# Rounding scales and normalisations as SCALAR_TENSOR_TENSOR, zeros written by ScalarE, and another order of the steps between two stages

## The chip, the cores and the metric

The kernel runs on one core of a Trainium2 chip. The core has five engines, each with its own instruction queue: TensorE (PE, matrix products; its weight loads are listed as PEld), VectorE (DVE), ScalarE (ACT), GpSimd (POOL) and SyncE (SP, which issues DMA transfers). They share the on-chip memory SBUF and the accumulation banks PSUM, and wait for one another by semaphores. The metric is the device time of one execution in microseconds; lower is better.

## The reference

Two layers in post-norm form on x of shape 16 x 512 x 256, float32 throughout. Reduced to what matters:

```python
x = layernorm(x + attention(x))        # 16 heads, latent size 32, rotary, causal softmax
x = layernorm(x + fp4_ffn(x))          # silu(gate) * up, then down; width 704
x = layernorm(x + recurrence(x))       # 512 steps of tanh(state @ tanh(a) + x_t @ b)
x = layernorm(x + channel_mix(x))      # sigmoid gate, squared relu

def fp4_quant_dequant(x):              # on activations and on weights, blocks of 16
    scale = maximum(max(abs(xb), axis=-1) / 6.0, 1e-12)
    idx = searchsorted(MID, abs(xb / scale))
    return GRID[idx] * sign(xb / scale) * scale

def layernorm(x):
    return (x - mean(x)) / sqrt(var(x) + 1e-5)
```

## The kernel before

**Stage 1, attention and FFN.** It goes through 16 batches. A batch has twelve slots: four groups of heads by three blocks of queries. A slot's chain is: scores on PE (L524), mask and row minimum on DVE in one operation (L536, which writes `p` and `nm`), exp on ACT (L549), transposes on PE (L559), copies to SBUF on ACT (L561), the weighted sum on PE (L590), and a division (L573, L604 to L611). Between the slots of one batch, other steps are taken from a list written by hand (`PLAN`, with variants for batches 0, 1 and 15; `Beside.half_slot` takes them): latents and rotary products of the next batch (L457, L473, L476), the output projection of the batch before with its layernorm (`out_projection`), and that batch's FFN: rounding of the rows (`quantize`), gate and up products (`ffn_up`), rounding of the hidden rows, and the down product with its layernorm (`ffn_down`). All of it works on blocks of 128 rows; a batch has four.

**Order.** PE's order is that in which the program is written (`tc.manual_schedule` for PE). The orders of DVE, ACT, POOL and SP are made by a scheduler, from data dependences and from costs, so an instruction that is taken out or costed in another way moves its neighbours. PSUM banks rotate over a pool of seven.

**fp4 rounding** (`fp4`, L183 to L215) is called 142 times: 74 times on 256 columns of activations or weights with 128 rows, twice with 64 rows, and 66 times on 704 columns. Its operations are: L201 the block maxima, L202 the scale with its lower bound, L203 the reciprocal, L204 a factor 1 - 2^-23 on the reciprocal, L207 the product with the rows, L209 and L210 the exponent, L213 the addition that rounds (all DVE), and L214 the subtraction and L215 the product with the scale (POOL). The buffers `q_sc`, `q_inv`, `q_q`, `q_m` exist twice.

**Layernorm.** `stats_into` (L91, L92, DVE) gives mean and variance, `rstd_of` (L84, L86, POOL) the factor, and one DVE instruction with two values for each row subtracts and multiplies: L98 in `layernorm` (after the FFN, 64 times) and L502 in `out_projection` (after the attention, 64 times, in pairs).

**Between the stages.** After the last slot only batch 15's output projection and FFN are left, and stage 2 cannot begin before its first rows are done. `FIRST` is a list of steps that sets PE's order there: E quantizes the rows of a block (`quantize_now`), U is one call of `ffn_up` (transposes, then two halves of the products), D one of `ffn_down`, F takes one DVE step of a hidden block's rounding, N is `normed`, the RMS norm and transposes of the recurrence's first rows. The number is the block (or pair).

**Stage 2** is the recurrence: 512 steps, PE products L1020 and L1060, tanh on ACT into `hist` (L1068), with channel mix, read-out and the last layernorm of earlier rows beside it.

**Zeroed buffers.** `vpad` (two of 128x2048, L400) is zeroed by POOL in the prologue, `hist` (four of 128x1024, L1008) by POOL at the start of the transition. `ta` (128x1024) holds tanh(a) and is ready long before.

Of the kernel before, what the change touches and what calls it, by code (L numbers as in the profile page):

```python
# [10 lines left out]
F32 = mybir.dt.float32  # L11
# [3 lines left out]
AF = mybir.ActivationFunctionType  # L15
ALU = mybir.AluOpType
# [3 lines left out]
P = 128  # L20
B, T, C = 16, 512, 256
# [38 lines left out]
def tile_kernel(ctx: ExitStack, tc: tile.TileContext, I: dict, out: bass.AP):  # L60
    nc = tc.nc


    const = ctx.enter_context(tc.tile_pool(name="const", bufs=1))
# [3 lines left out]
    make_identity(nc, ident)  # L68
    neg_half = const.tile([P, 4], F32, name="neg_half")
    nc.gpsimd.memset(neg_half, -0.5)  # L70
    cols = const.tile([P, NCOLS], F32, name="cols")
    nc.sync.dma_start(cols, I["cols"])

# [7 lines left out]
    def rstd_of(mv, n, eps):  # L81

        ve = small.tile([P, 4], F32, tag="ve", name="ve")
        nc.gpsimd.tensor_scalar(ve[:, :n], mv[:, :n, 1], 1.0, eps, ALU.mult, ALU.add)  # L84
        rs = small.tile([P, 4], F32, tag="rstd", name="rstd")
        nc.gpsimd.tensor_tensor(rs[:, :n], ve[:, :n], neg_half[:, :n], ALU.pow)  # L86
        return rs

    def stats_into(mv_slice, x):
        st = small.tile([P, 6], F32, tag="bnst", name="bnst")  # L90
        nc.vector.bn_stats(st, x)  # L91
        nc.vector.bn_aggr(mv_slice, st)  # L92

    def layernorm(dst, src):
        mv = small.tile([P, 4, 2], F32, tag="mv", name="mv")
        stats_into(mv[:, 0, :], src)
        rs = rstd_of(mv, 1, LN_EPS)
        nc.vector.tensor_scalar(dst, src, mv[:, 0, 0:1], rs[:, 0:1], ALU.subtract, ALU.mult)  # L98

# [46 lines left out]
    def mm(name):  # L148
        banks.append(banks.pop(0))
        return banks[-1].tile([P, 512], F32, tag="mm", name=name)  # L150
# [30 lines left out]
    def fp4(dst, x, nb, rows=P):  # L181

        n = nb * 16
        sc = ffn.tile([P, 44], F32, tag="q_sc", name="q_sc", bufs=2)[:rows, :nb]  # L190
        inv = ffn.tile([P, 44], F32, tag="q_inv", name="q_inv", bufs=2)[:rows, :nb]
        q = ffn.tile([P, FF], F32, tag="q_q", name="q_q", bufs=2)[:rows, :n]
        m = ffn.tile([P, FF], F32, tag="q_m", name="q_m", bufs=2)[:rows, :n]

        def blocks(t):
            return t.rearrange("p (n k) -> p n k", k=16)

        def over(t):
            return t.unsqueeze(2).to_broadcast([rows, nb, 16])

        nc.vector.tensor_reduce(sc, blocks(x), AX.X, ALU.max, apply_absolute_value=True)  # L201
        nc.vector.tensor_scalar(sc, sc, 1.0 / 6.0, 1e-12, ALU.mult, ALU.max)  # L202
        nc.vector.reciprocal(inv, sc)  # L203
        nc.vector.tensor_scalar(inv, inv, 1.0 - 2.0**-23, None, ALU.mult)  # L204
        if n > C:
            yield
        nc.vector.tensor_tensor(blocks(q), blocks(x), over(inv), ALU.mult)  # L207
        yield
        nc.vector.tensor_scalar(m.bitcast(U32), q.bitcast(U32), 0x7F800000, None, ALU.bitwise_and)  # L209
        nc.vector.tensor_scalar(m, m, 1.0, 1.5 * 2.0**22, ALU.max, ALU.mult)  # L210
        if n > C:
            yield
        nc.vector.tensor_tensor(q, q, m, ALU.add)  # L213
        nc.gpsimd.tensor_tensor(q, q, m, ALU.subtract)  # L214
        nc.gpsimd.tensor_tensor(blocks(dst), blocks(q), over(sc), ALU.mult)  # L215

    def ffn_weights():
# [20 lines left out]
        for r in range(2):  # L238
            w = ffn.tile([P, FF], F32, tag="h", name="w", bufs=2)
            nc.sync.dma_start(w, I["w_down"][r * P : r * P + P, :])  # L240
            wq4 = ffn.tile([P, FF], F32, tag="hq", name="wq4", bufs=2)
            for _ in fp4(wq4, w, FF // 16):
                pass
            yield 0.3
            for k0 in (0, 3):
                ps = mm("ps_t")
                for kb in range(k0, k0 + 3):
                    (of, n), at = PARTS[kb], (kb - k0) * P
                    nc.tensor.transpose(ps[:n, at : at + P], wq4[:, of : of + n], ident)
                    nc.scalar.copy(wdT[:n, kb, r * P : r * P + P], ps[:n, at : at + P])  # L250
                yield 1.5
# [89 lines left out]
    with ExitStack() as a:  # L341
# [54 lines left out]
            )  # L396

        vpad = [wts.tile([P, NT, H, 32], F32, name=f"vpad{i}") for i in range(2)]
        for i in range(2):
            nc.gpsimd.memset(vpad[i], 0.0)  # L400

# [78 lines left out]
        def out_projection(b):  # L482
            while b not in whole:
                yield None
            x, yT = x_of[b], y_of.pop(b)
            for j in range(0, NT, 2):
                mv = small.tile([P, 4, 2], F32, tag="mv", name="mv")
                ps = mm("ps_o")
                for i in range(2):
                    for hf in range(2):  # L490
                        nc.tensor.matmul(
                            ps[:, i * C : i * C + C],
                            yT[:, hf, (j + i) * P : (j + i) * P + P], cpT[:, hf, :],
                            start=hf == 0, stop=hf == 1,
                        )
                both = x[:, j : j + 2, :].rearrange("p j c -> p (j c)")
                nc.vector.tensor_tensor(both, ps, both, ALU.add)
                for i in range(2):
                    stats_into(mv[:, i, :], x[:, j + i, :])
                rs = rstd_of(mv, 2, LN_EPS)  # L500
                for i in range(2):
                    nc.vector.tensor_scalar(  # L502
                        x[:, j + i, :], x[:, j + i, :], mv[:, i, 0:1], rs[:, i : i + 1],
                        ALU.subtract, ALU.mult,
                    )
                yield 0.9

# [190 lines left out]
        with tc.manual_schedule(engines={mybir.EngineType.PE}), ExitStack() as s:  # L698
# [8 lines left out]
            rows = prep.tile([1, C], F32, name="rows")  # L707
# [74 lines left out]
        ps_b = five.enter_context(tc.tile_pool(name="ps_b", bufs=5, space=PSUM))  # L782
        ps_y = five.enter_context(tc.tile_pool(name="ps_y", bufs=1, space=PSUM))
        banks[:] = [ps_2] * 2 + [ps_b] * 5

        with tc.manual_schedule(engines={mybir.EngineType.PE}):
            slots = [(b, g, n) for b in range(B) for g in range(4) for n in range(len(BLOCKS))]
# [3 lines left out]
            for slot in slots + [None]:  # L791
                if slot:
                    b, g, n = slot
                    if g == 0 and n == 0:
# [5 lines left out]
                        if b == 2:  # L800
                            ta, wb, wc, bout = recurrent_weights()
# [176 lines left out]
    def value(p):  # L978
# [24 lines left out]
    hist = [  # L1003
        [wts.tile([P, 8, 2, 64], F32, name=f"hist{g}{i}") for i in range(2)] for g in range(2)
    ]
    for g in range(2):
        for i in range(2):
            nc.gpsimd.memset(hist[g][i], 0.0)  # L1008
    state = [None, None]
    clean, ot_of = {}, {}  # L1010

# [63 lines left out]
    def beside(M):  # L1075
# [14 lines left out]


    FIRST = [
        "E3", "U0", "U0", "E1", "U0", "U3", "U1", "U1", "D0", "E2", "F0", "D0", "U1", "U2", "N0",
        "U2", "U3", "F1", "U2", "N0", "F2", "U3",
    ]
    LATER = {
        0: [
# [23 lines left out]
    with tc.manual_schedule(engines={mybir.EngineType.PE}):  # L1121
# [40 lines left out]
        for t in range(T):  # L1162
# [9 lines left out]
            for g in range(2):  # L1172
                if us[g] is None or us[g][0] + us[g][1] == t:
                    t0, n = starts[g].pop(0)
# [9 lines left out]
            if t % 8 == 7:  # L1184
                at = t % 16 - 7
                for g in range(2):
                    old, new = hist[g][t // 8 % 2], clean[t // 16, g]
                    old = old.rearrange("p t k (r s b) -> p t k r s b", r=2, s=2)
                    for r in range(2):
                        rs, qs = slice(r * 64, r * 64 + 64), slice(64 - r * 64, 128 - r * 64)  # L1190
# [108 lines left out]
```

## Time and profile before

| | us |
|---|---|
| median of 3 runs | 2560.16 (2558.01 to 2562.15) |
| profiled execution, its own time | 2558.65 |
| its span in the profile | 2556.6 |
| prologue, up to the first scores | 31.0 |
| batches 0 and 1 | 98.7 and 111.1 |
| batches 2 to 14, each | 107.6 to 109.6 |
| batch 15 | 110.6 |
| transition, up to the recurrence's first product | 67.1 |
| recurrence | 728.3 |

A batch is counted from its first score product (L524) to that of the next; batch 15 ends, and the transition begins, with the last score product of all.

How to read the rows: a group of instructions has its line, engine, operation, output and inputs by the program's names, the shape, the number of instructions (x), then busy time in us, mean ns of one, and the idle time of the engine ahead of them with what ended it. A row of the timeline has the start in us, the length in us (of all its instructions, where there are several), engine and line; in brackets stands the engine's idle time before it and the instruction that released it. Instructions of one engine overlap at their ends, so the time from start to start can be shorter than the length.

### The profile page before, as it was taken

Reading aid. Unit: us, or ns where it says so; the run is one execution under the profiler, and the core shown is the slowest. Engines: PE = TensorE matmul, PEld = TensorE weight load, DVE = VectorE, ACT = ScalarE, POOL = GpSimd, SP = SyncE. Lnnn points to the kernel's source line nnn. Section 1 sums busy time; section 2 is a strip of 40 time slices with the busy share of each in tenths; the row PEclk is TensorE's granted clock in tenths of the full one; section 3 lists DMA queues with packets and bytes.
Section 4 is the critical chain, followed back from the end, with each engine's and each line's share of the span. In section 5 each row is a group of like instructions: output and inputs, shape, how many; then the busy total and the mean of one; then the engine's idle time right before and its main releaser. Section 6 shows DMA issues by size and latency. Waiting matters only on the chain.

```text
span 2556.6 us, 73922 instructions
## 1 busy us (share of the span) xinstructions
PE 2428.8 (95%) x28802; PEld 1713.3 (67%) x28802; DVE 1944.7 (76%) x5621; ACT 1613.2 (63%) x5532; POOL 1036.7 (41%) x1649
## 2 busy tenths in 40 slices
PE   8789999999999999999999999997799999999998
PEld 4456666666666666666666666665578888888885
DVE  6767888788888888888787887877756666666666
ACT  4656666666666666667666666664266666666664
POOL 4322333333333333333333333333545555555554
PEclk9889999999999999999999999999899999999999
DMA  3000000000000000000000000000101111111100
GB/s 118 22 10 6 14 22 14 16 15 12 24 14 16 16 12 24 14 16 14 14 16 22 14 14 7 16 11 11 42 28 40 40 40 40 38 38 40 36 28 27
DMA packets 58016, 61.30 MB, mean 24 GB/s; under 512 B 7873, under 2 KB 53058, under 8 KB 57666
## 3 DMA queue, kind: packets, MB, share of 16 engines
q1 hardware_dynamic: 56802, 55.54, 7.1%
q8 instruction: 226, 3.70, 0.6%
q14 instruction: 124, 1.02, 0.1%
q10 hardware_dynamic: 864, 1.05, 0.1%
HBM read 39.79 MB, written 16.78 MB: 22 GB/s over the span
## 4 chain that ended last, share of the span: by engine, by line
PE 54%; DVE 28%; ACT 9%; POOL 5%; issue 3%; DMA 1%; ACTq 0%; DVEq 0%; POOLq 0%
PE u L1060 8%; DVE p L536 6%; PE ps_pt L559 5%; PE u L1020 5%; PE S L524 4%; ACT p L549 4%; PE py L590 3%; PE pg L160 3%; PE pu L160 3%; PE ps_h L439 3%; ACT pT L561 3%; DVE q_q L207 2%; PE ps_a L904 2%; PE ps_d L160 2%; DVE q_sc L201 2%
## 5 line engine op out<-in xcount | busy, mean ns | idle before, releaser
L549 ACT ACTIVATE p<-p,nm 128x512 f32<-128x512 f32 (+3 forms) x1024 | 569.9, 561 | 520.1 <-DVE nm L536 516.1
L1068 ACT ACTIVATE hist<-u 64x64 f32<-64x64 f32 x2048 | 445.5, 218 | 235.1 <-PE u L1060 153.0
L536 DVE CUSTOM_DVE_ANT_0 p<-S,mask 128x512 f32<-128x512 f32 (+3 forms) x1024 | 443.7, 483 | 50.2 <-PE S L524 50.2
L559 PEld LDWEIGHTS ps_pt<-ident,p 128*128 128x128 f32 x2560 | 296.5, 141 | 235.4 <-issue 85.5
L1060 PEld LDWEIGHTS u<-hist,ta 128*64 128x64 f32 x8176 | 367.3, 138 | 119.9 <-ACT hist L1068 40.7
L559 PE MATMUL ps_pt<-ident,p 128*128 128x128 f32 x2560 | 393.3, 280 | 9.0 <-DVE nm L536 3.5
L1060 PE MATMUL u<-hist,ta 128*64 128x32 f32 x8176 | 394.2, 218 | 4.6 <-ACT hist L1068 4.4
L561 ACT COPY pT<-ps_pt 128x384 f32<-128x384 f32 (+1 forms) x768 | 370.0, 515 | 39.2 <-PE ps_pt L559 38.9
L214 POOL TENSOR_TENSOR q_q<-q_q,q_m 128x256 f32<-128x256 f32 (+1 forms) x142 | 167.3, 1178 | 452.0 <-DVE q_q L213 434.4
L524 PE MATMUL S<-kc,qr 32*128 32x128 f32 (+3 forms) x2048 | 235.3, 474 | 8.9 <-ACT qr L478 7.9
L1020 PE MATMUL u<-xt,wb 128*64 128x64 f32 x4128 | 223.0, 230 | 2.4 <-issue 2.4
L549 ACT ACTIVATION_READ_ACCUMULATOR p<-p,nm 128x1 f32 x1024 | 199.3, 195 | 0.0
L160 PE MATMUL pg<-wgT,xqT 128*128 128x352 f32 x512 | 177.6, 470 | 4.1 <-ACT xqT L289 2.9
L473 POOL TENSOR_TENSOR qc<-qc,qs 128x512 f32<-128x512 f32 x64 | 81.5, 1274 | 236.3 <-DVE qs L472 231.3
L160 PE MATMUL pu<-wuT,xqT 128*128 128x352 f32 x512 | 172.8, 460 | 1.2 <-DVE th L304 1.2
L160 PE MATMUL ps_d<-wdT,hT 128*128 128x256 f32 x732 | 169.7, 381 | 2.2 <-ACT hT L323 2.2
L590 PEld LDWEIGHTS py<-pT,vpad 128*32 128x32 f32 x5120 | 141.2, 110 | 43.0 <-issue 30.7
L1020 PEld LDWEIGHTS u<-xt,wb 128*64 128x64 f32 x4128 | 164.9, 138 | 7.4 <-issue 3.0
L590 PE MATMUL py<-pT,vpad 128*32 128x128 f32 x5120 | 165.3, 276 | 3.8 <-ACT pT L561 3.5
L524 PEld LDWEIGHTS S<-kc,qr 32*128 32x128 f32 x2048 | 110.8, 185 | 78.0 <-issue 32.0
L84 POOL TENSOR_SCALAR ve<-mv 128x1 f32<-128x1 f32 (+1 forms) x160 | 32.6, 204 | 302.1 <-DVE mv L92 276.7
L160 PEld LDWEIGHTS ps_d<-wdT,hT 128*128 128x128 f32 x732 | 134.9, 191 | 19.6 <-ACT hT L323 3.1
(164 smaller groups left out, 4595.6 us busy)
## 6 DMA issues: line engine op xcount, KB each, us to landing
xT<-in_xT_dram SPq DMA_DIRECT2D x16, 512.0 KB
x<-in_x_dram SPq DMA_DIRECT2D x16, 512.0 KB
xs<-x SPq DMA_DIRECT2D x64, 128.0 KB
x<-xs SPq DMA_DIRECT2D x32, 256.0 KB
xm<-xs SPq DMA_DIRECT2D x32, 256.0 KB
out_dram<-o SPq DMA_DIRECT2D x64, 128.0 KB
w<-in_w_down_dram SPq DMA_DIRECT2D x2, 352.0 KB
w<-in_w_gate_dram SPq DMA_DIRECT2D x5, 128.0 KB
```

The source lines that it names most:

```text
L160: nc.tensor.matmul(dst, left, right, start=start, stop=stop)
L214: nc.gpsimd.tensor_tensor(q, q, m, ALU.subtract)
L473: nc.gpsimd.tensor_tensor(of[k], of[k], x, ALU.add)
L524: nc.tensor.matmul(S[h][:, at : at + w], q[rs, i * P : i * P + P], k[rs, :w], start=True, stop=True,)
L536: nc.vector.tensor_tensor_reduce(out=p[:, own], in0=S[h][:, own], in1=mask[:, T - (i + 1) * P :], scale=1.0, scalar=-MASKED, op0=ALU.add, ...
L549: nc.scalar.activation(p[:, own], p[:, own], AF.Exp, bias=nm[:, u : u + 1], scale=-1.0, accum_out=sum_of[b, g][:, cb, half, h : h + 1],)
L559: nc.tensor.transpose(ps[:, at : at + P], p[:, at : at + P], ident)
L561: nc.scalar.copy(pT[:, :w], ps[:, :w])
L590: nc.tensor.matmul(py[q * 32 : q * 32 + 32, PLACE[i][1], :], vpad[b % 2][:, j, g * 4 + h, :], pt, start=j == 0 and h % 2 == 0, stop=j == i ...
L1020: nc.tensor.matmul(u[rs, k, par:n:2, bs : bs + 16], wb[:, g * 2 + k, par, half, rs], xt[:, g, at : at + n - par : 2, :], start=par == 0 an ...
L1060: nc.tensor.matmul(into[cs, :, c, :], ta[:, t % 2, g * 2 + k, cs], own[:, :, c, :], start=False, stop=True, skip_group_check=True,)
L1068: nc.scalar.activation(state[g][rs, :, r * 32 : r * 32 + 32].rearrange("p k (s b) -> p k s b", s=2), u[rs, :, t - t0, :] .rearrange("p k ( ...
```

## The change

1. In `fp4`, L202 becomes a SCALAR_TENSOR_TENSOR whose second operand is a constant tile `tiny` (128x44, set to 1e-12 once by POOL). L204 is taken out; its factor goes into L207, which becomes a SCALAR_TENSOR_TENSOR.
2. In `layernorm` and `out_projection` the TENSOR_SCALAR with two values for each row becomes a SCALAR_TENSOR_TENSOR: the mean as the per-row scalar, the factor as a tensor broadcast along 256 columns.
3. `vpad` is zeroed after the prologue's preparation in program order; on POOL this puts the small zeroing of `ones` ahead of it.
4. `hist` is zeroed by four ACT instructions: Identity of `ta` with scale 0.
5. `FIRST` has another order, with the same steps.

On the engines: DVE has 142 instructions fewer, POOL three fewer (four zeroings gone, one new), ACT four more; PE and SP have the same number. PE's order differs in the transition alone, SP's in one pair of loads of the prologue that change places. DVE's order differs around each rounding; the ACT and POOL orders differ by a few places for each batch.

```diff
@@
+    tiny = const.tile([P, 44], F32, name="tiny")
+    nc.gpsimd.memset(tiny, 1e-12)
@@ layernorm
-        nc.vector.tensor_scalar(dst, src, mv[:, 0, 0:1], rs[:, 0:1], ALU.subtract, ALU.mult)
+        nc.vector.scalar_tensor_tensor(
+            dst, src, mv[:, 0, 0:1], rs[:, 0:1].to_broadcast([P, C]), ALU.subtract, ALU.mult
+        )
@@ fp4
         nc.vector.tensor_reduce(sc, blocks(x), AX.X, ALU.max, apply_absolute_value=True)
-        nc.vector.tensor_scalar(sc, sc, 1.0 / 6.0, 1e-12, ALU.mult, ALU.max)
+        nc.vector.scalar_tensor_tensor(sc, sc, 1.0 / 6.0, tiny[:rows, :nb], ALU.mult, ALU.max)
         nc.vector.reciprocal(inv, sc)
-        nc.vector.tensor_scalar(inv, inv, 1.0 - 2.0**-23, None, ALU.mult)
         if n > C:
             yield
-        nc.vector.tensor_tensor(blocks(q), blocks(x), over(inv), ALU.mult)
+        nc.vector.scalar_tensor_tensor(
+            blocks(q), blocks(x), 1.0 - 2.0**-23, over(inv), ALU.mult, ALU.mult
+        )
@@ before the attention's preparation
         vpad = [wts.tile([P, NT, H, 32], F32, name=f"vpad{i}") for i in range(2)]
-        for i in range(2):
-            nc.gpsimd.memset(vpad[i], 0.0)
@@ out_projection
-                    nc.vector.tensor_scalar(
-                        x[:, j + i, :], x[:, j + i, :], mv[:, i, 0:1], rs[:, i : i + 1],
-                        ALU.subtract, ALU.mult,
+                    nc.vector.scalar_tensor_tensor(
+                        x[:, j + i, :], x[:, j + i, :], mv[:, i, 0:1],
+                        rs[:, i : i + 1].to_broadcast([P, C]), ALU.subtract, ALU.mult,
                     )
@@ after the attention's preparation
         banks[:] = [ps_2] * 2 + [ps_b] * 5
+        for i in range(2):
+            nc.gpsimd.memset(vpad[i], 0.0)
@@ stage 2
     for g in range(2):
         for i in range(2):
-            nc.gpsimd.memset(hist[g][i], 0.0)
+
+            nc.scalar.activation(
+                hist[g][i].rearrange("p t k n -> p (t k n)"), ta.rearrange("p a k n -> p (a k n)"),
+                AF.Identity, scale=0.0,
+            )
@@
     FIRST = [
-        "E3", "U0", "U0", "E1", "U0", "U3", "U1", "U1", "D0", "E2", "F0", "D0", "U1", "U2", "N0",
-        "U2", "U3", "F1", "U2", "N0", "F2", "U3",
+        "U0", "U0", "E1", "E3", "U0", "U3", "D0", "U1", "F0", "E2", "D0", "U1", "N0", "U2", "U1",
+        "F1", "U2", "U2", "U3", "U3", "F2", "N0",
     ]
```

## The prediction

> **What bounds the kernel now.** I read the page's totals and its chain, then the windows by stage, then the groups of the edited lines with shapes kept apart, and last the timeline where those lines stand.
>
> ```profile
> span 2556.6 us, 73922 instructions
> PE 2428.8 (95%) x28802; PEld 1713.3 (67%) x28802; DVE 1944.7 (76%) x5621; ACT 1613.2 (63%) x5532; POOL 1036.7 (41%) x1649
> PE 54%; DVE 28%; ACT 9%; POOL 5%; issue 3%; DMA 1%; ACTq 0%; DVEq 0%; POOLq 0%
> ```
>
> PE is busy 95% of the span, yet only 54% of the chain is PE: the other half is DVE (28%), ACT and POOL handing work to it. A shorter DVE instruction pays where it stands on that 28%. The windows below are one steady batch, the transition, and the recurrence (columns: length; busy us of PE, PEld, DVE, ACT, POOL; PE clock; DMA share; GB/s).
>
> ```profile
> 893.00:1001.00 108.00, 106.02 (x852) 70.78 (x853) 89.01 (x267) 71.13 (x213) 37.35 (x45) 1.00 0.05 16
> 1761.00:1828.00 67.00, 45.05 (x254) 31.18 (x246) 45.96 (x124) 13.94 (x42) 24.68 (x35) 0.87 0.09 28
> 1828.00:2557.00 729.00, 704.75 (x15206) 569.71 (x15206) 483.94 (x1253) 466.71 (x2112) 409.26 (x900) 0.99 0.13 36
> ```
>
> The recurrence is PE's (705 of 729 us) and none of its instructions changes. What can move is the sixteen batches (DVE 89 of 108 us) and the transition, where every engine has holes. The edited lines, and the nearest rows for their new form (busy us, mean ns, then idle before):
>
> ```profile
> L502 DVE TENSOR_SCALAR x<-x,mv,rstd 128x256 f32<-128x256 f32 x64 | 36.8, 615 | 29.1 <-POOL rstd L86 29.1
> L204 DVE TENSOR_SCALAR q_inv<-q_inv 128x16 f32<-128x16 f32 x74 | 31.2, 423 | 1.0
> L942 DVE SCALAR_TENSOR_TENSOR muk<-d,cols,x3T 128x256 f32<-128x256 f32 x64 | 28.0, 476 | 0.2
> L98 DVE TENSOR_SCALAR x<-x,mv,rstd 128x256 f32<-128x256 f32 x64 | 26.4, 413 | 74.1 <-POOL rstd L86 74.0
> L204 DVE TENSOR_SCALAR q_inv<-q_inv 128x44 f32<-128x44 f32 x66 | 24.0, 364 | 1.1
> ```
>
> The same TENSOR_SCALAR costs 413 ns at L98 and 615 at L502, and L204 has a mean of 423 and 364 ns where its median is 176. The timeline tells why:
>
> ```profile
> 923.04 0.73 POOL L214 TENSOR_TENSOR q_q<-q_q,q_m 128x256 f32<-128x256 f32 x1
> 923.11 1.50 DVE L502 TENSOR_SCALAR x<-x,mv,rstd 128x256 f32<-128x256 f32 x2 [0.86 <-POOL rstd L86]
> 926.23 1.12 PE L457 MATMUL ps_q<-heads,bdq 64*128 64x512 f32 x2 [0.40 <-DVE nm L536]
> ...
> 954.34 1.67 POOL L214 TENSOR_TENSOR q_q<-q_q,q_m 128x704 f32<-128x704 f32 x1 [0.90 <-DVE q_q L213]
> 954.46 1.59 DVE L204 TENSOR_SCALAR q_inv<-q_inv 128x16 f32<-128x16 f32 x1
> 956.08 0.42 DVE L207 TENSOR_TENSOR q_q<-x,q_inv 128x256 f32<-128x256 f32 x1
> ...
> 1779.27 3.61 POOL L1008 MEMSET hist<- 128x1024 f32 x4
> 1779.36 3.98 DVE L502 TENSOR_SCALAR x<-x,mv,rstd 128x256 f32<-128x256 f32 x2 [0.43 <-POOL rstd L86]
> ...
> 1788.40 0.69 PE L287 MATMUL ps_xq<-ident,xq 128*128 128x128 f32 x2 [10.20 <-POOL xq L215]
> ```
>
> A DVE instruction that starts just behind a POOL one ends when that one ends: L204 on 16 columns lasts 1.59 us beside a 1.67 us subtraction, an L502 pair 1.50 us beside L214 and L215, and 3.98 us beside four zeroings.
>
> **The change, part by part.** The profiled execution took 2558.65 us, 1.5 below the median of 2560.16; I sum against it and add the 1.5 at the end.
>
> *L204 removed (142 instructions, 56 us busy).* Sorted by length, 111 run free at 0.16 to 0.19 us; 31 wait behind POOL and hold 31 of the 56 us. A free one delays the next instruction by only 0.12 us (16 columns) to 0.19 (44), starts compared: 20 us in all. The waiting ones save less than they show, because L207 follows with two inputs in SBUF and two-input instructions wait too (L207 takes 1.33 us beside POOL's L473, L213 1.56 at 1804.51 beside L215). At 954.46 I give back nearly all of the 1.59.
>
> *L207 as SCALAR_TENSOR_TENSOR (142).* L991 is 711 ns on 512 columns where TENSOR_TENSOR L938 is 695: +0.016 each, 2 us. *L202 (142).* Bounds: 0 and the +0.06 of L942 over L98; at 16 or 44 columns I take +0.03, 4 us.
>
> *L98 and L502 (64 each).* Nearest row: L942, the same width and a per-row scalar, 476 against 413, so +0.063 each, 8 us of DVE; 0.5 us a batch. Free of POOL the L502 pair would be 0.73 before and 0.85 after, from start to end.
>
> *Another order on DVE*, made by the scheduler. In each batch's stretch around 915 to 926 (normalisation of one pair, rounding of the pair before) L213 of the first block moves behind the second L502 pair and one mask operation, so POOL's L214 and L215 come later and the pair runs alone: 1.50 becomes 0.85. Of that, PE's ps_q, which waits for the mask operation behind it, gets about 0.55 (0.4 to 0.8; it waited 0.40, and the exps before it also come earlier). POOL's rounding ends about 1 us later, with its transposes not due for several us.
>
> In the two stretches with a 704-wide rounding beside 512-wide scores (943 to 963, 969 to 990) a third mask operation goes behind L207 and a fourth behind L209, and in the second h (L307) goes behind L213. Gains: one L204 (0.19), less of L202's waiting (0.28 at 974.47, when POOL's work has moved). Losses: the mask operations 0.4 later, L307 0.75 later, with ps_h waiting on it already by 0.37. I take −0.2 and −0.3, from −0.6 to +0.7 each. Sum per batch: −0.55 −0.25 −0.3, less a few hundredths elsewhere: −1.05; thirteen steady batches −13.7, and the three irregular ones (0, 1, 15), where DVE has more room, −0.6.
>
> *Zeroing by ScalarE.* ACT is idle from 1774.4 to 1789.1; four ACTIVATEs of 128x1024 at 1.06 us (row L131) lie in it, if ACT comes to them at 1778, and the next ACT work is L289 at 1789.1. If L289 came 3 us earlier there would still be room. POOL sheds 3.6 us, and the L502 pair at 1779.36 falls from 3.98 to 0.85. *vpad's zeroing* goes behind one small zeroing of the prologue; POOL has no other work until 17 and vpad is first written at 42.8: nothing. On SP two loads of the prologue change places (the last rows of a weight before a piece of the recurrence's), the one that comes later first read by a matmul at 1857: nothing, at most the 0.6 us of one such transfer. *tiny* is one zeroing of 44 columns: nothing; POOL is free there.
>
> *FIRST.* U0 goes ahead of E1 and E3, D0 before U1, N0 to the end. First transposes (1788.40) come 2.1 earlier: 3.1 gained, 1.0 lost because the second pair now goes ahead of the first block's L209, L210 and L213. The h0 chain: U1's th and h no longer beside its rounding, but x2's L214 is put before it on POOL (+0.7): hq0's transposes (1805.85, 6.12 us of PE idle) −1.7. From D0 on PE has some 15 us of work and DVE as much; h2's and h3's roundings stand beside POOL's L867 and L909 (2.50 us), which now meet L209 and L210. I take the recurrence's first matmul at 1827.3 for 1828.31, before the batches' gain: −1, from −4 to +2.
>
> Sum: −13.7 −0.6 −1 = −15, less 1 for what the longer L98 adds on the path: −14. 2558.65 − 14 + 1.5 = **2546 us**.
>
> **The rivals.**
>
> *Slower: mask operations and h too late.* In the two 704-wide stretches PE's pg (951.17) waits for a bank that the third mask frees, and ps_h (980.34, already 0.37 late) for h. If each delay, 0.4 and 0.7, reaches PE in full, a batch loses 1.1 instead of gaining 0.55: with the first stretch's gain kept, +0.55 × 16 = +9, and 2569. Against it: L204 before them is gone. It decides from 0.28 us per stretch on.
>
> *The new form is dear.* From 256 to 704 columns L207 grows from 431 to 911 ns (1.07 a column), L209 unblocked from about 0.29 to 0.52 us (0.51 a column); two inputs cost twice the time a column. By slope, 256 columns would cost +0.14 instead of +0.063, and 128 of them +10 us on DVE, of which two thirds on the path: 2553. The direct row L942 speaks against it. The Trainium skill's "VectorE: DVE Perf Modes", § The perf-mode tier table, states that fp32 tensor_scalar in SBUF runs at twice the rate of tensor_tensor; by that rule the estimate is half of 256 cycles at its 0.96 GHz, +0.133 us an instruction and some 2552. L98 against L942 shows half of it.
>
> *The waits only change their name.* If L207 inherits all of L204's waiting and the new order's gains fall on time that PE did not wait, −2 remains: 2558, no change. For it: after L204 always comes a two-input instruction. Against: the L502 pair is freed by the order, not by the form. The Trainium skill's "SBUF — State Buffer", § Who interferes with whom, has two-input DVE instructions wait only for POOL instructions that read SBUF, and one-input ones in a fast mode for any; the memsets' 3.98 us and L207's 1.33 fit it, and by it the new form alone frees nothing beside L214 and L215.
>
> **How the numbers follow.** Likeliest 0.58 (2546; its own range 2535 to 2554), dear form 0.08, renamed waits 0.16, late masks 0.18. Low end: followed over the thirteen steady batches, the chain gives L204 35.6 us and L502 29.1; half of the first, the rest going to two-input waits, with 9 of the second (0.65 a pair) is −27, or 2533. High: 2567 takes in the nearer part of the late masks and leaves about 0.12 above; 0.06 lie below the low end. About 0.2% is what a measurement of this kernel can tell from no change. Faster than 2555: 0.57 + 0.06 + 0.03 = 0.66; slower than 2565.3: 0.16 + 0.02 = 0.18; the rest 0.16.
>
> **What would show it.** Right: no L204; L502 without any of 3 us and its pairs at 0.85; batches of 107 us for 108; ps_xq's 10.2 us wait near 8; the first u near 1812 (1828 less the batches' 14 and the transition's 1). Renamed waits: L202 and L207 with means over 0.6 and 1.1 us, and batches of 108. Late masks: PE waiting on nm and h by 0.5 us or more a batch in place of 0.40 and 0.37, batches over 108.5. Dear form: L98 above 0.52 us. I would be wrong most easily in the two 704-wide stretches, whose order I priced by offsets of 0.2 to 0.7 us, and in the transition.

## Result and profile after

The changed kernel takes 2543.97 us (median; 2542.90 to 2545.63) beside 2559.09 (2557.99 to 2562.15) for the kernel before on the same chip: a ratio of 0.994, 95% interval 0.9922 to 0.9957. It is faster by 0.6%; the forecast of 2546 is 2 us away. How far its terms hold is another question, and most of what follows is about that. The profiled execution took 2543.47 us, 15.2 less than the one the forecast was made from.

The page of the changed kernel, totals and chain:

```profile
span 2541.4 us, 73811 instructions
PE 2425.4 (95%) x28802; PEld 1719.8 (68%) x28802; DVE 1918.5 (75%) x5479; ACT 1616.0 (64%) x5536; POOL 1033.8 (41%) x1646
PE 60%; DVE 22%; ACT 10%; POOL 4%; issue 3%; DMA 1%; ACTq 0%; DVEq 0%; POOLq 0%
```

PE does the same 28802 products; DVE has 142 instructions less, and its share of the chain falls from 28% to 22%. The windows of the same steady batch, the transition and the recurrence (columns as before):

```profile
886.00:992.00 106.00, 105.33 (x852) 70.99 (x852) 87.22 (x258) 70.87 (x213) 37.37 (x45) 1.00 0.05 16
1746.00:1816.00 70.00, 45.19 (x245) 31.97 (x243) 42.83 (x120) 17.80 (x45) 24.57 (x34) 0.84 0.09 27
1816.00:2541.00 725.00, 704.01 (x15206) 569.99 (x15206) 482.48 (x1248) 466.72 (x2112) 404.70 (x897) 0.99 0.13 37
```

A batch takes 106 us in place of 108. The transition is 3 us longer and the recurrence 3 shorter. By stage, in us of one profiled execution each:

| | before | changed | difference |
|---|---|---|---|
| prologue | 31.0 | 31.9 | +0.9 |
| batches 0 and 1 | 209.8 | 210.9 | +1.1 |
| batch 2 | 109.1 | 109.9 | +0.8 |
| batches 3 to 14 | 1300.7 | 1279.1 | −21.6 |
| batch 15 | 110.6 | 113.8 | +3.2 |
| transition | 67.1 | 70.6 | +3.5 |
| recurrence | 728.3 | 725.1 | −3.2 |

So all of the gain lies in twelve equal batches. The edited lines there, groups with shapes kept apart (L205, L206, L207, L210, L214, L215, L218 are now the maxima, the scale, the reciprocal, the product, the two exponent steps and the rounding addition; POOL's two are L219 and L220; the masks L539):

```profile
L210 DVE SCALAR_TENSOR_TENSOR q_q<-h,q_inv 128x704 f32<-128x704 f32 x64 | 70.1, 1095 | 1.1
...
L210 DVE SCALAR_TENSOR_TENSOR q_q<-x,q_inv 128x256 f32<-128x256 f32 x64 | 42.3, 663 | 1.0
...
L100 DVE SCALAR_TENSOR_TENSOR x<-x,mv,rstd 128x256 f32<-128x256 f32 x64 | 31.0, 484 | 74.9 <-POOL rstd L88 74.9
...
L505 DVE SCALAR_TENSOR_TENSOR x<-x,mv,rstd 128x256 f32<-128x256 f32 x64 | 28.3, 481 | 30.3 <-POOL rstd L88 30.3
```

L100 was 413 ns, L505 615. The product grew from 911 to 1095 ns on 704 columns and from 431 to 663 on 256. The timeline shows where:

```profile
915.86 0.88 DVE L505 SCALAR_TENSOR_TENSOR x<-x,mv,rstd 128x256 f32<-128x256 f32 x2 [0.86 <-POOL rstd L88]
...
917.77 0.73 POOL L219 TENSOR_TENSOR q_q<-q_q,q_m 128x256 f32<-128x256 f32 x1 [1.94 <-DVE q_q L218]
918.35 1.12 PE L460 MATMUL ps_q<-heads,bdq 64*128 64x512 f32 x2
...
946.68 1.67 POOL L219 TENSOR_TENSOR q_q<-q_q,q_m 128x704 f32<-128x704 f32 x1
947.07 1.57 DVE L210 SCALAR_TENSOR_TENSOR q_q<-x,q_inv 128x256 f32<-128x256 f32 x1
...
1763.91 0.88 DVE L505 SCALAR_TENSOR_TENSOR x<-x,mv,rstd 128x256 f32<-128x256 f32 x2 [0.43 <-POOL rstd L88]
...
1770.90 0.69 PE L292 MATMUL ps_xq<-ident,xq 128*128 128x128 f32 x2 [8.15 <-POOL xq L220]
```

Three readings. The normalising pair now runs ahead of POOL's subtraction and takes 0.88 us where it took 1.50, and PE's ps_q behind it no longer waits. The 1.59 us that L204 waited beside a 704-wide subtraction are now 1.57 of L210 beside the same subtraction. And the pair at the start of the transition takes 0.88 in place of 3.98.

PE's waits in the steady batches (between 340 and 1650 us; total us, times, longest), the kernel before:

```profile
PE ps_q L457 <- ACT pT L561: 8.0, 13, 0.6
PE S L524 <- ACT qr L478: 6.5, 12, 0.5
PE ps_q L457 <- DVE nm L536: 4.8, 12, 0.4
PE ps_h L321 <- DVE h L307: 3.9, 12, 0.4
```

and the changed kernel:

```profile
PE S L527 <- ACT qr L481: 7.0, 13, 0.5
PE ps_h L326 <- DVE h L312: 2.9, 7, 0.7
PE ps_xq L292 <- DVE th L309: 1.5, 5, 0.4
```

Both waits at ps_q are gone: 0.4 us a batch behind a mask (the one I forecast) and 0.6 us a batch behind `pT`, which the forecast never named. The listed waits fall by about 12 us of the 21.6. The other 9 show no idle time: they stand in PE's busy time, which falls from 1271.9 to 1262.6 us in batches 3 to 14 for the same 10176 products. Products that overlap hide such a wait: one of a slot's eight score products can start late while the others run (experiment 4 shows one such place). Not all of the 9 us was followed to its place.

### The profile page after: what moved, and what is told of

It is laid out like the page before. It is cut to its first block, busy times and chain, and to the rows that moved or that the text cites. A ratio compares the mean times of both kernels' runs of the same rounds, so it can differ in the third digit from the quotient of the medians.

```text
span 2541.4 us, 73811 instructions
## 1 busy us (share of the span) xinstructions
PE 2425.4 (95%) x28802; PEld 1719.8 (68%) x28802; DVE 1918.5 (75%) x5479; ACT 1616.0 (64%) x5536; POOL 1033.8 (41%) x1646
## 4 chain that ended last, share of the span: by engine, by line
PE 60%; DVE 22%; ACT 10%; POOL 4%; issue 3%; DMA 1%; ACTq 0%; DVEq 0%; POOLq 0%
PE u L1069 8%; PE ps_pt L562 6%; PE u L1029 5%; PE S L527 5%; DVE p L539 5%; ACT p L552 4%; PE ps_d L164 4%; PE py L593 4%; PE pg L164 3%; PE pu L164 3%; ACT pT L564 3%; DVE q_q L210 2%; PE ps_a L909 2%; PE ps_h L442 2%; PE ps_k L909 2%
## 5 line engine op out<-in xcount | busy, mean ns | idle before, releaser
L539 DVE CUSTOM_DVE_ANT_0 p<-S,mask 128x512 f32<-128x512 f32 (+3 forms) x1024 | 442.6, 483 | 53.2 <-PE S L527 53.2
L219 POOL TENSOR_TENSOR q_q<-q_q,q_m 128x256 f32<-128x256 f32 (+1 forms) x142 | 166.6, 1174 | 422.7 <-DVE q_q L218 420.6
```

The costliest lines, as they stand in the source:

```text
L539: nc.vector.tensor_tensor_reduce(out=p[:, own], in0=S[h][:, own], in1=mask[:, T - (i + 1) * P :], scale=1.0, scalar=-MASKED, op0=ALU.add, ...
```

## Experiments

Each is one edit of the kernel before, or the changed kernel with one edit taken back. Ratios are to the kernel before on the same chip. "b3–14" is batches 3 to 14, "trans" the transition, "rec" the recurrence; 1300.7, 67.1 and 728.3 us in the kernel before. Line numbers in the quoted rows are those of the kernel named.

**1. The factor in the product alone.**

```diff
-        nc.vector.tensor_scalar(inv, inv, 1.0 - 2.0**-23, None, ALU.mult)
...
-        nc.vector.tensor_tensor(blocks(q), blocks(x), over(inv), ALU.mult)
+        nc.vector.scalar_tensor_tensor(
+            blocks(q), blocks(x), 1.0 - 2.0**-23, over(inv), ALU.mult, ALU.mult
+        )
```

> Only the factor 1 - 2^-23 moves from L204 into L207 (142 instructions fewer on DVE); normalisations, L202, zeroing and FIRST as before. Theory (the batches gain because L204 is gone and because the scheduler, with it gone, puts L213 behind the second L502 pair): batches 2 to 14 lose 1.2 to 1.8 us each, the whole kernel 15 to 22 us; L502's mean falls from 615 to under 480 ns. Rival (L207 inherits the waits of L204): batches 2 to 14 within 0.4 us of before, the whole within 5 us, L207's waiting as long as L204's was.

Measured: 2537.2 us, 0.9911 (0.9897 to 0.9924); b3–14 1274.7, trans 67.0, rec 731.3. This one edit brings 26 us in the steady batches, more than the whole change and more than its theory expected. Of the rival only one half came true: the waits are renamed, as the groups show (L206 is its product):

```profile
L206 DVE SCALAR_TENSOR_TENSOR q_q<-h,q_inv 128x704 f32<-128x704 f32 x64 | 71.2, 1113 | 1.1
...
L206 DVE SCALAR_TENSOR_TENSOR q_q<-x,q_inv 128x256 f32<-128x256 f32 x64 | 43.1, 676 | 0.9
...
L503 DVE TENSOR_SCALAR x<-x,mv,rstd 128x256 f32<-128x256 f32 x64 | 26.9, 461 | 29.9 <-POOL rstd L86 29.9
```

The products take 28.6 us more than before ((1113 − 911) × 64 + (676 − 431) × 64), of the 31 that L204 spent waiting. The pair of L503 stands free (461 ns for 615) although its form is the old one: it is the order on DVE that freed it.

**2. The same, with the 142 instructions left standing.** The old multiplication is still issued, but writes a tile that nobody reads.

```diff
+    dead = const.tile([P, 44], F32, name="dead")
...
-        nc.vector.tensor_scalar(inv, inv, 1.0 - 2.0**-23, None, ALU.mult)
+        nc.vector.tensor_scalar(dead[:rows, :nb], inv, 1.0 - 2.0**-23, None, ALU.mult)
```

> The factor moves from L204 into L207 as in the fold alone, but the 142 small TENSOR_SCALAR instructions stay on DVE: they read the reciprocal and write a tile that nothing reads. Theory (about two thirds of the fold's 23 us are the instructions' own issue and time on DVE, 0.12 to 0.19 us each plus their waits, and a third is order and a shorter dependence): ratio 0.997 to 1.000, batches 2 to 14 at 1400 to 1411 us. Rival (the gain is the other order and the shorter chain of rounding): ratio 0.991 to 0.994, batches near 1385.

Measured: 2539.5 us, 0.9923 (0.9910 to 0.9935); b3–14 1278.7.

```profile
L208 DVE SCALAR_TENSOR_TENSOR q_q<-h,q_inv 128x704 f32<-128x704 f32 x64 | 56.7, 886 | 0.0
...
L205 DVE TENSOR_SCALAR dead<-q_inv 128x16 f32<-128x16 f32 x74 | 31.5, 425 | 1.0
...
L205 DVE TENSOR_SCALAR dead<-q_inv 128x44 f32<-128x44 f32 x66 | 27.2, 412 | 1.1
...
L208 DVE SCALAR_TENSOR_TENSOR q_q<-x,q_inv 128x256 f32<-128x256 f32 x64 | 26.6, 416 | 0.0
```

The small instructions are as long as ever (425 and 412 ns, 58.7 us in all) and take the waits back from the product (886 and 416). Still only 4.0 of the 26 us return: the theory (a ratio of 0.997 to 1.000) missed, and the rival holds. The small instructions and the products together take 142 us, where they took 141 in the kernel before, and most of the gain stays. What this kernel has in common with the one of experiment 1, and not with the kernel before, is that the multiplication is no longer a link between the reciprocal and the product, and that the product has its new form. I argue that the scheduler sees a shorter chain and so orders DVE in another way. How it decides is not shown, and the new form of the product with the old chain left as it was has not been run, so the form as the cause of the new order is not ruled out.

**3. The order alone.** The kernel before, with edges that only order DVE's instructions for the scheduler and make nobody wait at a semaphore: the 256-wide rounding addition behind the second normalisation of the pair; in the second kernel, whose diff follows, also `h` behind the 704-wide addition.

```diff
+    def order_after(made, last):
+        if last[0] is not None:
+            tc.add_manual_dep(
+                made.ins, last[0].ins.name,
+                mybir.DependencyInfo(mybir.DependencyClass.NoSync, mybir.DependencyReason.DATA),
...
-        nc.vector.tensor_tensor(q, q, m, ALU.add)
+        added = nc.vector.tensor_tensor(q, q, m, ALU.add)
+        if n > C:
+            last_add[0] = added
+        else:
+            order_after(added, last_norm)
...
-                    nc.vector.scalar_tensor_tensor(h[:, fs], th, 0.5, ps[:, :352], ALU.mult, ALU.mult)
+                    made = nc.vector.scalar_tensor_tensor(
+                        h[:, fs], th, 0.5, ps[:, :352], ALU.mult, ALU.mult
+                    )
+            order_after(made, last_add)
```

> The kernel before, every instruction as it was (L204 too), with one rule of order on DVE: L213 of a 256-wide block goes behind the second L502 pair, as in the changed kernel. Theory (the order, not the instructions, gives the gain of the first stretch, which the fold moved by 0.9 us a batch): L502's mean falls from 615 to about 465 ns, batches 2 to 14 together 7 to 12 us shorter, the whole 6 to 12 us faster, ratio 0.995 to 0.998. Rival (it takes the shorter chain of rounding too): the pair is freed and the batches stay within 3 us of 1410.

> As the run with one rule of order, and a second rule: L307 of the next block goes behind L213 of the 704-wide rounding before it, so that POOL's L214 and L215 start earlier; L204 and everything else as before. Theory (the second rounding of the stretch cannot pass POOL's work on the first): another 0.5 to 0.9 us a batch, the whole 12 to 20 us faster than before, ratio 0.992 to 0.995, close to the run with the idle small instructions. Rival (L204 itself, in the chain, is what costs): no faster than with one rule.

Measured: one edge 2561.87 us, 1.0010 (1.0001 to 1.0018), b3–14 1296.1, batch 15 117.0; both 2558.65, 0.9994 (0.9985 to 1.0003), b3–14 1293.4, batch 15 115.8. PE's waits between 340 and 1650 us with the first edge:

```profile
PE ps_q L470 <- ACT pT L574: 7.4, 12, 0.6
...
PE ps_h L334 <- DVE h L320: 3.5, 12, 0.4
```

and with both:

```profile
PE ps_h L339 <- DVE h L322: 6.8, 7, 1.3
PE ps_q L475 <- ACT pT L579: 4.3, 9, 0.6
```

Both theories missed: they had expected 6 to 12 and 12 to 20 us of the whole. The first edge removes the mask wait at ps_q, all of it, and brings 4.6 us in the steady batches; batch 15 takes 6.4 back, so the whole is no faster. Within a batch the first ps_q comes 0.64 us earlier, the score products behind it only 0.27, at the place that experiment 4 shows, and the end of the batch 0.38 (means of batches 3 to 14). The second edge brings 2.7 more: 3.1 of the wait on `pT` go, though `h`, now later, costs 3.3 more at ps_h, so the listed waits do not account for the 2.7. Two moves by hand therefore carry 7.3 of 22 to 26 us, without a single instruction less. Experiment 2 leaves little for the instructions themselves, so I put the remainder down to the other moves that the scheduler makes in the same stretches. That is argued by exclusion; they were not tried one by one, and it stays open which of them carry it.

How the wait on `pT` goes can be read in the stretch with two 704-wide roundings, one behind the other, near the end of a batch. DVE in the kernel before (the batch starts at 892.93):

```profile
976.45 0.68 DVE L536 CUSTOM_DVE_ANT_0 p<-S,mask 128x512 f32<-128x512 f32 x1
...
977.06 0.88 DVE L207 TENSOR_TENSOR q_q<-h,q_inv 128x704 f32<-128x704 f32 x1
...
980.21 0.88 DVE L213 TENSOR_TENSOR q_q<-q_q,q_m 128x704 f32<-128x704 f32 x1
...
984.39 1.01 DVE L207 TENSOR_TENSOR q_q<-h,q_inv 128x704 f32<-128x704 f32 x1
...
987.37 0.55 DVE L536 CUSTOM_DVE_ANT_0 p<-S,mask 128x384 f32<-128x384 f32 x1
```

and in the changed kernel (the batch starts at 885.97):

```profile
968.01 0.88 DVE L210 SCALAR_TENSOR_TENSOR q_q<-h,q_inv 128x704 f32<-128x704 f32 x1
968.81 0.68 DVE L539 CUSTOM_DVE_ANT_0 p<-S,mask 128x512 f32<-128x512 f32 x1
...
971.34 0.88 DVE L218 TENSOR_TENSOR q_q<-q_q,q_m 128x704 f32<-128x704 f32 x1
...
974.54 1.88 DVE L210 SCALAR_TENSOR_TENSOR q_q<-h,q_inv 128x704 f32<-128x704 f32 x1
...
978.39 0.55 DVE L539 CUSTOM_DVE_ANT_0 p<-S,mask 128x384 f32<-128x384 f32 x1
```

The masks of the next slots (the 384-wide ones) stand behind the second rounding's addition in both. From the start of the batch they come at 94.44 us before (987.37 − 892.93) and at 92.42 now (978.39 − 885.97). Behind them follow the exps, the copies of `pT`, and ps_q: 97.52 before and 95.51 now (a gain of 2.0; the mean of the twelve batches is 1.8). Of these 2.0 us, 0.92 were already there at the first ps_q and 1.12 at the maxima that open the first rounding here. Then the first product goes ahead of a 512-wide mask, which had stood before it (0.6), and the scale and L204 in front of it hold it up less (0.4): it starts at 82.04 against 84.13. The addition keeps 1.9 of this. It passes `h`, but a mask has come in between, so that swap alone gains it little. POOL's subtraction and product for the first rounding follow 1.9 us earlier in the batch (86.33 against 88.23), and the second rounding waits behind them mostly in one place, L210 (1.88 us), where L202 and L204 had waited one after the other (0.93 and 0.97 us). That the product passes a mask is one of the moves that neither edge makes.

**4. The new form at the two normalisations.** Alone, and the changed kernel with the old form there.

```diff
-        nc.vector.tensor_scalar(dst, src, mv[:, 0, 0:1], rs[:, 0:1], ALU.subtract, ALU.mult)
+        nc.vector.scalar_tensor_tensor(
+            dst, src, mv[:, 0, 0:1], rs[:, 0:1].to_broadcast([P, C]), ALU.subtract, ALU.mult
+        )
...
-                    nc.vector.tensor_scalar(
-                        x[:, j + i, :], x[:, j + i, :], mv[:, i, 0:1], rs[:, i : i + 1],
-                        ALU.subtract, ALU.mult,
+                    nc.vector.scalar_tensor_tensor(
+                        x[:, j + i, :], x[:, j + i, :], mv[:, i, 0:1],
+                        rs[:, i : i + 1].to_broadcast([P, C]), ALU.subtract, ALU.mult,
```

> Only L98 and L502 become SCALAR_TENSOR_TENSOR; L204 stays. The scheduler puts L213 behind the second L502 pair here too. Theory (the order frees the pair, 0.55 us a batch to PE, the form costs 0.06 an instruction): L502 at 0.47 to 0.49 us with none over 0.6, L204 as before, batches 2 to 14 down by 0 to 0.5 us each, the whole 0 to 8 us faster. Rival (the form is what matters, because its instructions no longer wait for POOL): the gain is most of the 15 us of the whole change. Rival (dear form): L98 above 0.52 us and the whole slower by 3 us or more.

> The changed kernel with TENSOR_SCALAR at both normalisations. Theory (the new form costs 0.066 us an instruction, eight a batch, all of it on the path): batches 2 to 14 together 5 to 8 us shorter than the changed kernel's 1389, the whole 5 to 8 us faster than the changed kernel, ratio about 0.991. Rival (the form frees instructions from POOL and so pays): L502's mean rises above 0.55 us and the batches are no shorter than 1389.

Measured: alone 2563.5 us, 1.0009 (1.0000 to 1.0017), b3–14 1301.4; the changed kernel without it 2536.57, 0.9911 (0.9897 to 0.9924), b3–14 1274.6, where the changed kernel has 1279.1 and, run again, 1280.2. The theory for the first kernel missed, that for the second held. So in the changed kernel the new form costs 4.5 to 5.6 us in these batches. Each of their 96 instructions is 0.07 longer (413 to 484 ns at the first; 410 and 481 at the second, both free of POOL), 6.8 in all, but the price is not spread over them evenly. It arises at one place of the batch, first in the changed kernel (the batch starts at 885.97), then without the new form (it starts at 883.72):

```profile
924.13 0.74 DVE L470 SCALAR_TENSOR_TENSOR kc<-ps_k,cols,cos 128x512 f32<-128x512 f32 x1
924.38 1.45 PE L527 MATMUL S<-kc,qr 32*128 32x384 f32 x8
...
921.43 0.74 DVE L468 SCALAR_TENSOR_TENSOR kc<-ps_k,cols,cos 128x512 f32<-128x512 f32 x1
922.10 1.03 PE L525 MATMUL S<-kc,qr 32*128 32x384 f32 x8
```

One of the eight score products starts just behind the end of `kc`, 38.94 us from the start of the batch against 38.51 (`kc` ends at 38.89 and 38.45), while the others run, so the eight take 1.45 us for 1.03 and PE shows no idle time. These 0.4 us a batch then stay as they are for 46 us. `kc` stands on DVE behind three of the longer normalisations, which account for about 0.2; another order of a mask and the 256-wide addition there adds about 0.1. So length and order both have a share, and no run separates them. Alone, the new form frees the pair as well (481 ns, and no wait on a mask at ps_q), and ps_q comes 0.76 us earlier, but at this score product nothing of it is left (means of batches 3 to 14): the steady batches are no shorter.

The one thing the form buys is seen where POOL zeroes `hist`, in the first of the two kernels:

```profile
1784.71 3.61 POOL L1010 MEMSET hist<- 128x1024 f32 x4
1784.80 0.88 DVE L504 SCALAR_TENSOR_TENSOR x<-x,mv,rstd 128x256 f32<-128x256 f32 x2 [0.43 <-POOL rstd L86]
...
1786.26 2.09 DVE L204 TENSOR_SCALAR q_sc<-q_sc 128x16 f32<-128x16 f32 x1
```

The pair with two inputs runs through beside four POOL instructions that only write; the next TENSOR_SCALAR, on 16 columns, lasts until their end. Of the 3.1 us that the pair gains, 1.8 are left over transition and recurrence together (793.6 for 795.4).

**5. Zeroing by ScalarE.** Alone, and together with experiment 1.

```diff
-            nc.gpsimd.memset(hist[g][i], 0.0)
+            nc.scalar.activation(
+                hist[g][i].rearrange("p t k n -> p (t k n)"), ta.rearrange("p a k n -> p (a k n)"),
+                AF.Identity, scale=0.0,
+            )
```

> Only the zeroing of hist moves from POOL to ScalarE. Theory: the L502 pair in the transition falls from 3.98 to 0.75 us, ps_xq's wait from 10.2 to 7 us, the transition becomes 2 to 3 us shorter and the whole 2 to 3 us faster. Rival (something else in the transition ends last): the wait at ps_xq falls, the transition stays within 1 us of 67.1 and the whole within 1 us.

> The fold and the zeroing of hist by ScalarE, nothing else of the change. Theory (the fold's 0.9911 and the zeroing's 0.9995 add): ratio 0.989 to 0.991, 1 to 3 us faster than the fold alone and 7 to 10 us faster than the whole change; transition 65 to 66 us. Rival (what the transition gains is given back in the recurrence): ratio 0.991 to 0.992.

Measured: alone 2559.52 us, 0.9995 (0.9986 to 1.0004), trans 65.7, rec 728.6; with the factor in the product 2535.51, 0.9908 (0.9892 to 0.9923), b3–14 1275.6, trans 65.3, rec 731.7. Alone, the timeline reads:

```profile
1780.60 3.90 ACT L1009 ACTIVATE hist<-ta 128x1024 f32<-128x1024 f32 x4 [3.88 <-PE ps_o L491]
1781.68 0.73 DVE L502 TENSOR_SCALAR x<-x,mv,rstd 128x256 f32<-128x256 f32 x2 [0.43 <-POOL rstd L86]
...
1788.52 0.69 PE L287 MATMUL ps_xq<-ident,xq 128*128 128x128 f32 x2 [8.00 <-POOL xq L215]
```

The pair is free (0.73 for 3.98), the four zeroings lie in ACT's idle time, and the first transposes wait 8.00 us for 10.20. Of these 2.2 us, 1.4 are left at the recurrence's first product and 1.1 at the end. The others go in small steps behind it, at the up products and the first down product; PE's wait for the first hidden block's rounding is 6.1 us in both kernels. One us is less than the interval can tell from nothing.

**6. The order of the steps between the stages.** The new list in the kernel before, and the old one in the changed kernel.

```diff
-        "E3", "U0", "U0", "E1", "U0", "U3", "U1", "U1", "D0", "E2", "F0", "D0", "U1", "U2", "N0",
-        "U2", "U3", "F1", "U2", "N0", "F2", "U3",
+        "U0", "U0", "E1", "E3", "U0", "U3", "D0", "U1", "F0", "E2", "D0", "U1", "N0", "U2", "U1",
+        "F1", "U2", "U2", "U3", "U3", "F2", "N0",
```

> Only FIRST has the new order. Theory from the profile after (transition 3.5 us longer though its zeroing is gone from POOL): the transition gets 4 to 6 us longer, the recurrence 2 to 4 us shorter, the whole 1 to 3 us slower; batches 0 to 14 unchanged within 1 us. Rival (the longer transition comes from the other edits): transition within 1 us of 67.1, the whole within 1 us.

> The changed kernel with FIRST in its old order. Theory (the new order of FIRST costs in the transition, as it did alone: 7.8 us longer there, 4.9 us in the whole): the transition is 4 to 8 us shorter than the changed kernel's 70.6, the whole 3 to 7 us faster than the changed kernel, at a ratio of 0.991 to 0.993 to before. Rival (the new order was made for the edited operations and pays beside them): the whole is no faster than the changed kernel, ratio 0.994 or above.

Measured: the new list alone 2566.6 us, 1.0019 (1.0010 to 1.0028), trans 74.9 and rec 727.8, together 7.3 more than before. The changed kernel with the old list: 2547.04, 0.9957 (0.9944 to 0.9969), trans 65.5 and rec 734.9, together 4.7 more than the changed kernel. So the new list costs in one company and gains in the other; the theory for the second kernel missed, and its rival holds. PE's waits in the transition, new list alone:

```profile
PE ps_h L321 <- POOL hq L215: 9.7, 1, 9.7
```

and the changed kernel with the old list, from 1808 to 1835 us:

```profile
PE ps_xn L888 <- POOL xn L872: 7.3, 2, 4.0
```

With the new list PE waits 9.7 us for `hq` of the first block (6.1 before, 9.5 in the changed kernel): one pair of U1's products, 2.6 us of work that filled this time, now stands behind D0, and in the new list alone `hq` is later too, with x2's subtraction ahead of its product on POOL. The recurrence begins later, with all its first rows ready. With the old list it begins some 5 us earlier, but PE stands 4.0 us after two steps and 3.3 after two more for the normalised rows of the second pair, which wait on POOL and DVE behind the last two hidden blocks' roundings. In the kernel before this wait (on the same tiles) is 1.8 us over the whole span, with the factor alone (experiment 1) 5.3: the old list's weakness shows only once the roundings have moved.

**7. Three parts together, and the whole again.** The factor in the product, zeroing by ScalarE and the new list on the kernel before; then the changed kernel itself, on the same chip.

> The fold, the zeroing by ScalarE and the new FIRST; L202 and both normalisations as before, vpad as before. Theory (of the change the normalisations' new form costs 6 to 7 us and the rest pays): ratio 0.990 to 0.991, 6 to 9 us faster than the whole change beside it; the recurrence's first second-pair tokens are no longer late, so transition and recurrence together are 1 to 2 us shorter than with the old FIRST. Rival (the old FIRST is better here, as it was alone): 2 us or more slower than the fold with the zeroing, ratio 0.992.

> The changed kernel itself, beside the others on one chip. Expected ratio 0.993 to 0.995, as measured before, with batches 2 to 14 at 1387 to 1391 us.

Measured: three parts 2541.85 us (2535.56 to 2543.47), 0.9923 (0.9909 to 0.9936), b3–14 1274.7, trans 70.2, rec 725.7; the whole 2542.12, 0.9933 (0.9921 to 0.9946), b3–14 1280.2. The steady batches are again 5.5 us better without the new normalisations, but the prologue with batches 0 to 2 is 4 longer (355.5 for 351.7), so the whole misses the ratio that was expected; these stages vary from 346.8 to 355.5 over all kernels, and the cause is open. Beside the factor and the zeroing, the new list makes transition and recurrence together 1.1 us shorter (795.9 for 797.0 in experiment 5).

The fastest are the factor alone (0.9911), with ScalarE's zeroing (0.9908), and the changed kernel with the old normalisations (0.9911). They are 0.2% to 0.3% below the changed kernel (0.9940 and 0.9933), with intervals that just touch, and are not told apart from one another.

## Why the prediction was right, and where it was not

*The first stretch of a batch, −0.55 (0.4 to 0.8).* Right in mechanism and nearly in size: the order alone gives −0.64 at ps_q, and the pair takes 0.88 for the forecast 0.85. In the changed kernel ps_q comes 0.92 earlier, a little above the range. That the score products behind it give part back (with the order alone 0.27 of the 0.64 are left there) was not foreseen.

*The two 704-wide stretches, −0.25 and −0.3.* The sign was right, the size was half: together −1.1 (from −0.92 at the first ps_q to −2.01 at the second). The step that failed is the price of the new order there. It was booked as a loss: "the mask operations 0.4 later, L307 0.75 later, with ps_h waiting on it already by 0.37". `h` goes behind the addition, and PE does wait up to 0.7 for it, but only seven times and 2.9 us in all (3.9 before). The product that passes a mask helped to start POOL's half of the rounding 1.9 us earlier, a gain that the sum does not have, and what was late at the end of that stretch was not ps_h but the 384-wide masks behind the second rounding, whose wait at ps_q (8.0 us in 13 waits) the prediction does not name. So −13.7 for batches 2 to 14 measured −20.8.

*L204, "20 us in all" for the free ones and little for those that wait.* The waiting moved on as I said: 26.6 us of the 31 went to L210 ((1095 − 911) × 64 + (663 − 431) × 64). The instructions matter less than the starts suggest: those kept in b3–14, eight a batch and 96 in all, the waiting ones among them, cost 4.0 us there, or about 0.04 each where I had 0.12 and 0.19 for a free one. I had counted only one such per 704-wide stretch, so the sum was hardly touched.

*L98 and L502, +0.063 each.* Measured +0.071, in line with the row L942. The estimate of +0.133 by the Trainium skill's "VectorE: DVE Perf Modes", § The perf-mode tier table, is too high; the runs show about half of it. The term that was mis-sized is its share of the path: "less 1 for what the longer L98 adds on the path", on top of a few hundredths in the first stretch, and it was 4.5 to 5.6 in batches 3 to 14 alone, with a share for the order that the form brings.

*The three irregular batches, −0.6.* Wrong: +2.6, −1.5 and +3.2, together +4.3 (in experiment 7's run of the same kernel +2.1, +0.9 and +1.8, together +4.8). "Where DVE has more room" was no argument. In batch 15 the late masks came true, as in experiment 1's timeline:

```profile
1711.33 1.30 DVE L206 SCALAR_TENSOR_TENSOR q_q<-h,q_inv 128x704 f32<-128x704 f32 x1
1712.64 0.65 DVE L537 CUSTOM_DVE_ANT_0 p<-S,mask 128x512 f32<-128x512 f32 x1
```

The mask now stands behind a product that waits for POOL, where before it went ahead of it. In the changed kernel's batch 15 PE waits for row minima up to 1.9 us at once and 2.6 in all, where it had waited 1.2. Where the rest of the 3.2 lies, and what moved batches 0 and 1, is open.

*ScalarE's zeroing.* Right: hidden (3.90 us in ACT's hole), ps_xq's wait 8.15 where I said near 8. *vpad, tiny and the two loads on SP* were not tried singly; the prologue is 0.9 longer, and it varies by more than that between kernels.

*FIRST, −1 from −4 to +2.* The start of the recurrence was 1816.29 where I said 1812, so the term was +3.5 for −1. The first transposes did come 2.0 earlier in the transition, as forecast. What failed is the path behind them. The transposes of `hq` come 1.1 earlier, but from there to the recurrence's first product it takes 27.1 us for 22.5, where the forecast left room for less than one more: the pair of U1's products now lies there, and with N0 at the end of the list the last wait is 5.2 us for 2.4. But the recurrence's first rows are then all ready, and the recurrence is 3.2 shorter, which I had not considered. The two together are +0.3. In these two stages the list alone costs 7 us, and taking it back costs 5, so this term could not have been had from the kernel before alone.

*The sum.* −14 was forecast and −15.2 measured: batches 2 to 14 gave 7 more than their term even after paying for the new normalisations, and the irregular batches took 5 of it back. That the total is so close is in part luck, since the two misses have opposite signs.

*The rivals.* "Renamed waits" is true of the rows (L210 at 1095, near the forecast 1.1) and false of the time: which instruction waits matters little, what stands behind it in the queue matters. "Late masks" decided in batch 15 alone; the steady batches' mask wait at ps_q went to nothing. "Dear form" is refuted as a duration (0.484, limit 0.52), while its price on the path came near what that rival feared. Of the rule in the Trainium skill's "SBUF — State Buffer", § Who interferes with whom, the runs agree with both halves: one-input TENSOR_SCALARs wait for POOL whatever it does (2.09 us beside the zeroings, 1.59 beside the subtraction), two-input instructions only where POOL reads (1.57 beside the subtraction, 0.88 for a pair beside the zeroings).

## What to carry to other kernels

Where a scheduler orders an engine, price a removed instruction by what the new order makes early or late, not by its duration: here the 96 instructions of the steady batches hold 4 us of 26. List every wait of the bounding engine in a steady stage and follow each back to the end of the queue that releases it; the largest wait that went here, ps_q behind `pT`, is released by ACT, with transposes, an exp and a mask between it and the edited rounding. Try the parts of a change singly and taken back, since one part (the normalisations) cost a quarter of a per cent that the rest hid, and another (the list) changed its sign with its company.

## What the runs showed that was not expected

A small DVE instruction that sits in front of a long one costs almost nothing while both must wait for POOL anyway: with 58.7 us of them left standing over the whole span, the kernel is only 4.0 us slower in its steady batches, because the waiting merely changes its place (425 and 412 ns in the small ones with 886 and 416 in the products, against 1113 and 676 in the products alone).

A start of the recurrence that is 5 us earlier can make it end 5 us later: it runs into rows that are not yet normalised, and the 7.3 us it then stands still are counted in the recurrence, not in the transition. Times of single stages must be read together with the next one.

A wait can stand in an engine's busy time. Of eight overlapping score products one starts 0.4 us late, PE shows no gap, and the batch is 0.4 us longer at that point; in the steady batches 9 us of the gain lie in PE's busy time, though its products are the same.
